# A graph layer's segment sums on TensorE: 256 result columns in place of 128, except in the last ten groups

## The chip, the core and the metric

The kernel runs on one core of a Trainium2 chip. The metric is the device time in microseconds (us) from launch to end of one execution. Before the change three runs took 2691.51, 2695.5 and 2681.98 us; the median is 2691.51 us.

The engines are called by the profile's names: PE is TensorE (its weight loads are PEld), DVE is VectorE, ACT is ScalarE, POOL is GpSimd and SP is SyncE. A "q" behind a name is the engine's sequencer.

## What is computed

One message-passing layer of a graph network, a residual and a layer norm, all in fp32. There are 12500 nodes with 64 features and 212500 edges with 32 features, sorted by destination. Every edge runs through a two-layer MLP, the messages are summed by destination, and every node runs through another MLP:

```python
msg_in = jnp.concatenate([nodes[row], nodes[col], edge_features], axis=-1)
messages = _mlp(msg_in, mW1, mb1, mW2, mb2)
aggregated = jax.ops.segment_sum(messages, col, num_segments=nodes.shape[0])
upd_in = jnp.concatenate([nodes, aggregated], axis=-1)
...
x = _layernorm(x + _L0_gnn_ref(x, src, dst, edge_attr_32, ...), axis=-1)
```

`_mlp` is `relu(x @ W1 + b1) @ W2 + b2`. The kernel sums the hidden layer of the messages (128 wide) by destination and multiplies by `mW2 @ uW1` afterwards, once per node.

## The kernel before, in words

**Groups and tiles.** The edges are cut into 554 groups (`G`) of 384, each of three tiles (`TG`) of 128 edges. Since edges are sorted by destination, all destinations of a group lie in a window of 32 nodes (`W`). Four groups share one block of edge features (`SB`).

**What happens to a group g.**

- `gather` (L142, POOL): one indirect DMA for each tile (L145) fetches the 64 source features of 128 edges into `own.s[g % RING]`. There are 20 such buffers (`RING`). Gathers are issued 16 groups ahead in program order (`AHEAD`), and the first gather of a group waits for ACT's copy of the group 20 earlier (`copy_by[g - RING]`).
- `onehot` (L321, DVE): one comparison (L324) writes a 128x32 matrix of ones and zeros for each tile, saying which node of the window an edge goes to, behind the 64 features in the same buffer.
- `turn` (L354, PE): three transposes (L360) bring features and one-hot matrix to edge-per-column form in PSUM; ACT copies them to `own.st` (L372).
- `hidden` (L381, PE): one matmul for each tile (L392, two instructions each in the profile) makes the hidden layer; ACT applies the ReLU (L401) into `own.h`.
- `sums` (L411, PE): a small transpose (L419), then one matmul for each tile (L422, again two instructions each) that adds the hidden vectors up by destination. The result has 128 hidden rows and 32 columns of nodes; DVE adds it to `agg` (L431) and counts (L432).
- For 52 groups (`COPIED`), the third tile isn't gathered: DVE (L349) or ACT (L350) copies its 128 source columns one by one out of a transposed node table `xc` on the chip, spread over the steps before. Such a group has two gathers in place of three and two more matmuls in `hidden`.

**The repeated columns.** The moving operand of the sums' matmul is the 32-column one-hot matrix, read `TIMES` = 4 times over through a broadcast, so that the result has 4 x 32 = 128 columns, all four copies alike. Only the first copy (`sg[:, 0, :]`) is read. The places behind it in the same PSUM bank, the count line (`TIMES * W`) and the windows' products (`(TIMES + 1) * W`), are set by the same constant.

**Steps.** `step` (L502) puts work of several groups into one uninterrupted stretch on PE. In iteration k of the main loop (L536) it is `turn(k)`, `hidden(k - 2)`, `sums(k - 4)`, in that order. The first instruction of a step waits for all that the step needs, and only the last one signals. On that signal ACT copies group k (L372) and applies the ReLU for k - 2 (L401), and DVE adds the sums for k - 4 (L431, L432). Two PSUM sets (`own.ps[k % 2]`) alternate, so step k waits for what ACT and DVE did with step k - 2, and for `onehot(k)`. Every fourth step ends with one more matmul (`windows`, L310), which DVE copies in four pieces (L315); every fourth iteration also has DVE copy four windows (`places`, L303).

**Order on each engine.** The program is written in the order in which each engine executes it; there is no scheduler. DVE's order in an iteration is `onehot(k + 1)`, the two adds of step k, then any pieces of windows and copied columns. ACT's is copy, ReLU, copied columns. Every 512 nodes, an update (L438 to L483) runs the node MLP between steps: L449, L450 and L462 on PE.

**The end.** In the last ten groups (`SHORT`), the three parts are steps of their own, so that they follow each other without the distance of two iterations.

`unordered` (L584) is a way for inputs that break the assumptions, and isn't executed here.

Of the kernel before, what the change touches and what calls it, by code (L numbers as in the profile page):

```python
# [22 lines left out]
D = 64  # L23
# [5 lines left out]
W = 32  # L29
TG = 3  # L30
GE = TG * P
G = (E + GE - 1) // GE
# [12 lines left out]
SHORT = 10  # L45
# [3 lines left out]
COPIED = {**dict.fromkeys(BY_DVE, (ET.DVE, BY_DVE)), **dict.fromkeys(BY_ACT, (ET.Activation, BY_ACT))}  # L49
SLACK = 3  # L50
REGS = 8
TIMES = 4


def tiles_of(g):

    n = min(GE, E - g * GE)
    return [min(P, n - j * P) for j in range((n + P - 1) // P)]
# [46 lines left out]
def ordered(ctx: ExitStack, tc: tile.TileContext, a, own, ok):  # L105
# [25 lines left out]
    def after(first, *others):  # L131

        tc.declare_no_dep(first.ins, group="quiet", reason="waits for the last of a step")
        for i in others:
            tc.add_manual_dep(
                first.ins, i.ins.name,
                mybir.DependencyInfo(mybir.DependencyClass.Sync, mybir.DependencyReason.DATA),
                reason="the kernel's own rings",
            )
        return first  # L140
# [165 lines left out]
    def windows(b, wp, own_bank=True):  # L306


        xw, n = xws.pop(b)
        did = nc.tensor.matmul(wp[: n * W, :], xw[:, :n, :], w1b, start=True, stop=True)  # L310

        def copies():
            for i in range(n):
                g = b * SB + i
                c = nc.vector.tensor_copy(wm[g % NW][D : D + W, :], wp[i * W : (i + 1) * W, :])  # L315
                after(c, *([did] if own_bank else []), *([hidden_by[g - NW]] if g >= NW else []))
                wm_by[g] = c

        return did, copies
# [91 lines left out]
    def sums(g, ps):  # L411
        h, s = own.h[g % NH], own.s[g % RING]
        sizes = tiles_of(g)
        sg = ps[:, 2, : TIMES * W].rearrange("p (t w) -> p t w", w=W)


        lo = D if sizes[-1] == P else 0
        line = ps[0:1, 2, TIMES * W :][:, : D + W - lo]
        did = [nc.tensor.transpose(line, counts[lo:, g : g + 1], ident[lo : D + W, lo : D + W])]  # L419
        line = line[:, D - lo :]  # L420
        for j, p in enumerate(sizes):
            did.append(nc.tensor.matmul(  # L422
                sg, h[:p, j, :],
                s[:p, j, D:].unsqueeze(1).to_broadcast([p, TIMES, W]),
                start=j == 0, stop=j == len(sizes) - 1))

        def add(step):
            sums_by[g] = step
            at = bass.ds(starts.pop(g), W)
            return [  # L430
                after(nc.vector.tensor_tensor(agg[:, at], sg[:, 0, :], agg[:, at], ALU.add), step),  # L431
                after(nc.vector.tensor_tensor(xc[D : D + 1, at], line,  # L432
                                              xc[D : D + 1, at], ALU.add), step),
            ]

        return did, [*relu_by[g], copy_by[g]], add
# [53 lines left out]
    def step_update(g):  # L490
# [5 lines left out]
        elif now:  # L496
            got = now[1](now[0])
            now = [got, *now[2:]] if len(now) > 2 else []

    users = {part: [[], []] for part in (turn, hidden, sums)}  # L500

    def step(*work):  # L502
# [10 lines left out]
        for part, g, *_ in parts:  # L513
            if part is sums:
                for b in [b for b in xws if (b - 1) * SB <= g][:1]:
                    last, copies = windows(b, own.ps[g % 2][:, 2, (TIMES + 1) * W :][:, :H])
                    did.append(last)
# [18 lines left out]
    for k in range(G):  # L536
        if k < BITS:
            bit(k)
        if k % SB == 2:
            inputs(k // SB + 2)  # L540
        if k % SB == 1:
            places(k // SB + 1)
        onehot(k + 1)
        if k < G - SHORT:
            step((turn, k), *([(hidden, k - 2)] if k > 1 else []),
                 *([(sums, k - 4)] if k > 3 else []))
            made, summed = max(0, k - 1), max(0, k - 3)
        else:

            step((turn, k))  # L550
            for _ in range(2):
                if summed < made:
                    step((sums, summed))
                    summed += 1
            for _ in range(2):
                if made <= k:
                    step((hidden, made))
                    made += 1
        if k + AHEAD < G:
            gather(k + AHEAD)  # L560
        copies_of(k)
# [334 lines left out]
```

## Time and profile before

| | before |
|---|---|
| runs | 2691.51, 2695.5, 2681.98 us |
| profiled execution, its own time | 2690.72 us |
| its span, first to last instruction | 2688.9 us |
| mean granted PE clock | 0.787 |
| PE busy | 1687.1 us, 63% |
| POOL busy | 1519.4 us, 57% |
| DVE busy | 1060.2 us, 39% |
| ACT busy | 827.3 us, 31% |
| sums' matmuls L422 | 3322 instructions, 647.5 us |
| gathers L145 | 1609 instructions, 1518.6 us, 944 ns each |

A span of 2688.9 us over 554 groups is 4.85 us for a group. No engine is busy all the time, so the table alone doesn't say what sets this pace. Matmuls are pipelined: the mean time of one (343 ns) includes its way through the array, so the distance between the starts of two is shorter than that. The view of waits tells what ended the idle time in front of an instruction, and the timeline gives the start of every instruction in us from the start of the span.

### The profile page before, as it was taken

Reading aid. Unit: us, or ns where it says so; the run is one execution under the profiler, and the core shown is the slowest. Engines: PE = TensorE matmul, PEld = TensorE weight load, DVE = VectorE, ACT = ScalarE, POOL = GpSimd, SP = SyncE. Lnnn points to the kernel's source line nnn. Section 1 sums busy time; section 2 is a strip of 40 time slices with the busy share of each in tenths; the row PEclk is TensorE's granted clock in tenths of the full one; section 3 lists DMA queues with packets and bytes.
Section 4 is the critical chain, followed back from the end, with each engine's and each line's share of the span. In section 5 each row is a group of like instructions: output and inputs, shape, how many; then the busy total and the mean of one; then the engine's idle time right before and its main releaser. Section 6 shows DMA issues by size and latency. Waiting matters only on the chain.

```text
span 2688.9 us, 45023 instructions
## 1 busy us (share of the span) xinstructions
PE 1687.1 (63%) x9545; PEld 1457.1 (54%) x9545; DVE 1060.2 (39%) x7163; ACT 827.3 (31%) x4455; POOL 1519.4 (57%) x1616
## 2 busy tenths in 40 slices
PE   1356666666666675766666656666566666677667
PEld 0355555555555565655555555555555555565555
DVE  4124344344443444443434434434344343443423
ACT  0123333333333333333333333333333333333322
POOL 7565555555555555555555555555555555565550
PEclk9777787778777777777777878787777777787779
DMA  3211111111111111111111111111111111111110
GB/s 80 58 44 32 35 32 36 31 36 32 35 37 32 34 34 35 31 36 32 37 31 35 34 32 34 34 34 34 35 32 34 33 37 31 35 35 35 33 34 14
DMA packets 71878, 95.29 MB, mean 35 GB/s; under 512 B 32633, under 2 KB 40076, under 8 KB 71596
## 3 DMA queue, kind: packets, MB, share of 16 engines
q0 software_dynamic: 51488, 52.80, 10.3%
q1 hardware_dynamic: 19193, 39.06, 5.3%
q8 instruction: 81, 1.33, 0.2%
q14 instruction: 202, 1.65, 0.2%
q10 hardware_dynamic: 914, 0.46, 0.1%
HBM read 88.90 MB, written 3.20 MB: 34 GB/s over the span
## 4 chain that ended last, share of the span: by engine, by line
PE 50%; issue 18%; another core or an unknown queue 16%; ACT 10%; ACTq 3%; DVE 3%; DMA 0%; DVEq 0%; SPq 0%
PE own_ps L422 19%; PE own_ps L392 16%; PE own_ps L360 9%; ACT own_h L401 3%; ACT own_f L350 3%; ACT own_st L372 3%; ACTq L343 2%; PE own_ps L419 2%; PE u_ps L462 2%; PE u_ps L449 1%; PE own_ps L310 1%; ACTq L350 1%; PE u_ps L450 1%; DVE agg L431 1%
## 5 line engine op out<-in xcount | busy, mean ns | idle before, releaser
L145 POOL DMA_INDIRECT own_s<-in_x,src_sb x1609 | 1518.6, 944 | 1091.0 <-ACT own_st L372 677.1
L360 PE MATMUL own_ps<-own_ident,own_s 128*96 128x128 f32 x1661 | 364.2, 341 | 906.5 <-issue 677.0
L372 ACT ACTIVATE own_st<-own_ps 96x384 f32<-96x384 f32 (+2 forms) x606 | 286.1, 472 | 1697.7 <-PE own_ps L422 1006.0
L360 PEld LDWEIGHTS own_ps<-own_ident,own_s 128*96 128x96 f32 x1661 | 224.4, 159 | 983.9 <-issue 735.6
L422 PE MATMUL own_ps<-own_s,own_h 128*128 128x128 f32 x3322 | 647.5, 343 | 0.4 <-issue 0.3
L392 PE MATMUL own_ps<-own_wm,own_st 128*128 128x128 f32 (+1 forms) x3322 | 630.8, 338 | 1.4 <-DVE own_wm L315 1.4
L392 PEld LDWEIGHTS own_ps<-own_wm,own_st 128*128 128x128 f32 (+1 forms) x3322 | 571.9, 251 | 16.5 <-issue 11.7
L431 DVE TENSOR_TENSOR agg<-own_ps,agg 128x32 f32 x554 | 105.2, 190 | 1202.7 <-ACT own_h L401 1089.6
L422 PEld LDWEIGHTS own_ps<-own_s,own_h 128*128 128x128 f32 x3322 | 525.6, 236 | 27.3 <-issue 0.3
L349 DVE COPY own_f<-xc 64x1 f32 x3968 | 428.8, 143 | 217.7 <-issue 213.2
L350 ACT ACTIVATE own_f<-xc 64x1 f32 x2688 | 304.6, 193 | 9.1 <-issue 6.2
L401 ACT ACTIVATE own_h<-own_ps 128x384 f32<-128x384 f32 x553 | 263.3, 476 | 18.4 <-PE own_ps L392 13.1
L315 DVE COPY own_wm<-own_ps 32x128 f32<-32x128 f32 x550 | 156.9, 285 | 6.8 <-issue 1.3
L324 DVE TENSOR_TENSOR own_s<-iota,dlc 128x96 f32<-128x96 f32 x554 | 135.7, 245 | 21.6 <-issue 16.7
L432 DVE TENSOR_TENSOR xc<-own_ps,xc 1x32 f32 x554 | 101.2, 183 | 27.8 <-PE u_ps L450 7.4
L419 PE MATMUL own_ps<-own_ident,own_counts 32*1 32x32 f32 x554 | 107.1, 193 | 4.2 <-ACT own_st L372 1.9
L372 ACT ACTIVATION_READ_ACCUMULATOR own_st<-own_ps 96x1 f32 (+1 forms) x554 | 106.4, 192 | 0.6
L303 DVE COPY xw<-xc 66x32 f32 x554 | 78.6, 210 | 49.2 <-issue 48.3
L419 PEld LDWEIGHTS own_ps<-own_ident,own_counts 32*1 32x1 f32 x554 | 41.3, 74 | 93.8 <-issue 47.8
L310 PE MATMUL own_ps<-w1b,xw 66*128 66x128 f32 (+1 forms) x276 | 56.9, 290 | 0.0
L462 PE MATMUL u_ps<-u,u 128*128 128x64 f32 (+1 forms) x196 | 49.1, 398 | 10.0 <-ACT u L452 10.0
L462 PEld LDWEIGHTS u_ps<-u,u 128*128 128x128 f32 (+1 forms) x196 | 47.5, 326 | 11.5 <-ACT u L452 11.3
(63 smaller groups left out, 338.5 us busy)
## 6 DMA issues: line engine op xcount, KB each, us to landing
own_st<-in_efT SPq DMA_DIRECT2D x138, 192.0 KB
own_s<-in_x,src_sb POOLq DMA_INDIRECT x1609
xin<-in_x SPq DMA_DIRECT2D x24, 128.0 KB
out<-o SPq DMA_DIRECT2D x24, 128.0 KB
xc<-in_xT SPq DMA_DIRECT2D x12, 179.2 KB
dlc_i<-in_dst_cols SPq DMA_DIRECT2D x1, 831.0 KB
xc<-in_xT SPq DMA_DIRECT2D x4, 179.5 KB
src_sb<-in_src SPq DMA_DIRECT2D x13, 50.5 KB
```

Of the source, the lines that this page charges most:

```text
L145: nc.gpsimd.indirect_dma_start(out=s[:p, j, :D], out_offset=None, in_=x[:, :], in_offset=bass.IndirectOffsetOnAxis(ap=src_sb[:p, g * TG + ...
L315: c = nc.vector.tensor_copy(wm[g % NW][D : D + W, :], wp[i * W : (i + 1) * W, :])
L324: places_by[g] = nc.vector.tensor_tensor(own.s[g % RING][:, :, D:], iota.unsqueeze(1).to_broadcast([P, TG, W]), dlc[:, g * TG : (g + 1) * ...
L349: c = (nc.vector.tensor_copy(*column) if engine == ET.DVE else nc.scalar.activation(*column, AF.Copy))
L350: else nc.scalar.activation(*column, AF.Copy))
L360: nc.tensor.transpose(xt[:, j * P : j * P + p], s[:p, j, :], ident[:p, :p])
L372: nc.scalar.activation(t[to, c : c + m], xt[to, :m], AF.Copy, **({"accum_out": counts[to, g : g + 1]} if to.stop > D else {})), step)
L392: did.append(nc.tensor.matmul(pre[:p, j, :], edges, weights, start=i == 0, stop=i == len(parts) - 1))
L401: relu_by[g] = [nc.scalar.activation(h, pre, AF.Relu)]
L419: did = [nc.tensor.transpose(line, counts[lo:, g : g + 1], ident[lo : D + W, lo : D + W])]
L422: did.append(nc.tensor.matmul(sg, h[:p, j, :], s[:p, j, D:].unsqueeze(1).to_broadcast([p, TIMES, W]), start=j == 0, stop=j == len(sizes) - 1))
L462: nc.tensor.matmul(o_ps[:p, k], u[:, k:q:n], u2, start=True, stop=True)
```

## The change

The constant goes from four to eight, so the moving operand of the sums' matmul has 256 columns in place of 128. In the last ten groups it stays at 128 columns through a second constant.

```diff
-TIMES = 4
+TIMES = 8
+FEW = 4
...
     def sums(g, ps):
         h, s = own.h[g % NH], own.s[g % RING]
         sizes = tiles_of(g)
-        sg = ps[:, 2, : TIMES * W].rearrange("p (t w) -> p t w", w=W)
+        times = TIMES if g < G - SHORT else FEW
+        sg = ps[:, 2, : times * W].rearrange("p (t w) -> p t w", w=W)
...
                 sg, h[:p, j, :],
-                s[:p, j, D:].unsqueeze(1).to_broadcast([p, TIMES, W]),
+                s[:p, j, D:].unsqueeze(1).to_broadcast([p, times, W]),
```

The count line and the windows' products move with `TIMES`: from column 128 to 256 and from column 160 to 288 of the same bank of 512 columns. The number and the order of the instructions are the same on every engine; 544 of the 554 groups have matmuls of 128x256 in place of 128x128.

## The prediction

> **What bounds the kernel now.** I began with busy time and slices on the page. PE is busy 63% of the span, nothing more, and its clock changes all the time.
>
> ```profile
> PE 1687.1 (63%) x9545; PEld 1457.1 (54%) x9545; DVE 1060.2 (39%) x7163; ACT 827.3 (31%) x4455; POOL 1519.4 (57%) x1616
> ...
> PEclk9777787778777777777777878787777777787779
> ```
>
> The second row is the granted clock in tenths. It is an average of two values: the trace's clock records know only full and half speed, in stretches of 3.4 us or multiples of it. So each PE stage has two prices.
>
> Next the waits: they name a circle in which ACT waits for PE, POOL for ACT, and PE mostly for nothing visible.
>
> ```profile
> ACT own_st L372 <- PE own_ps L422: 1006.0, 245, 8.2
> ...
> POOL own_s L145 <- ACT own_st L372: 677.1, 274, 8.7
> PE own_ps L360 <- issue: 677.0, 223, 10.0
> ```
>
> POOL's 274 waits of 2.5 us are one for each pair of groups. To see what closes the circle I read the timeline of one stretch, engine by engine: start, duration, engine, work, and in brackets the idle time before.
>
> ```profile
> 1037.69 1.65 PE L422 MATMUL own_ps<-own_s,own_h 128*128 128x128 f32 x6
> ...
> 1043.78 0.94 PE L422 MATMUL own_ps<-own_s,own_h 128*128 128x128 f32 x6
> ...
> 1046.41 0.94 PE L422 MATMUL own_ps<-own_s,own_h 128*128 128x128 f32 x6
> 1054.17 0.85 PE L360 MATMUL own_ps<-own_ident,own_s 128*96 128x128 f32 x3 [6.83 <-issue]
> ```
>
> ```profile
> 1046.45 0.94 POOL L145 DMA_INDIRECT own_s<-in_x,src_sb  x1 [0.30 <-issue]
> 1050.34 0.94 POOL L145 DMA_INDIRECT own_s<-in_x,src_sb  x1 [2.94 <-ACT own_st L372]
> ```
>
> ```profile
> 1048.99 0.87 ACT L372 ACTIVATE own_st<-own_ps 64x256 f32<-64x256 f32 x2 [5.48 <-remote]
> ```
>
> The step with the sums at 1043.78 is over at 1044.94, the next one at 1047.35. ACT starts on the first only at 1048.99, 4.05 us late. It isn't busy; PE's semaphore is recorded as rising at 1048.97. That moment is 1.6 us after POOL's last allowed gather ended at 1047.39: when that gather lands. Counted over the trace, of 356 steps where ACT stood waiting, 189 got their signal over 0.3 us late, and 161 of these within 0.2 us after a gather's landing; of 44 steps that ended after the landing of the group 19 ahead, none was late. And where gathers are over (the last is issued at 2610.4), signals come at once:
>
> ```profile
> 2623.83 0.94 PE L422 MATMUL own_ps<-own_s,own_h 128*128 128x128 f32 x6
> ...
> 2625.81 0.94 PE L422 MATMUL own_ps<-own_s,own_h 128*128 128x128 f32 x6
> ```
>
> ```profile
> 2624.80 0.49 ACT L372 ACTIVATE own_st<-own_ps 96x384 f32<-96x384 f32 x1 [1.72 <-PE own_ps L422]
> ...
> 2626.78 0.49 ACT L372 ACTIVATE own_st<-own_ps 96x384 f32<-96x384 f32 x1 [1.02 <-PE own_ps L422]
> ```
>
> There a step takes 1.98 us, against 4.75 in the middle. Why PE's signal waits for a landing I can't say; that it does sets the pace. A pair of groups costs 6 gathers x 1.247 us (start to start) + about 1.45 to the landing + about 0.6 for ACT's copy and POOL's start: 9.5 us. Measured from one pair's signal to the next: median 9.52 and 9.57, and about 8.2 where a copied group leaves five gathers. So **the bound is POOL's ring with its landing**, and PE work costs only where a step ends after the landing.
>
> **Where PE is late.** Steps fall into a rhythm of four. Call them by k mod 4. P (0) and Q (1) run at full clock and wait for the landing: P's signal comes a median 3.8 us after its work, Q's with it. Then PE idles (median 5.6 us before R) and drops to half clock. R (2) runs mostly at half clock (110 of 129 start there): its signal comes 0.0 us after its work in the median, so PE ends about with the landing or after it. S (3) follows at once, turns to full clock on its way, and signals promptly.
>
> **The change, part by part.**
>
> *Columns.* Six L422 instructions start 112 ns apart at full clock and 213 ns at half (1043.78 and 1037.69 above). L449 with 512 columns starts 853 ns apart at half clock, four times the 213 ns: time goes with columns. So 256 columns add 6 x 213 = 1.28 us at half clock and 6 x 112 = 0.67 us, say 0.64, at full. Weighted with the clock that each step had, that is 0.86 us in the mean and 443 us in all. If all of it were on the path: 2690.7 + 443 = 3134 us; if none: 0. The weights (L422 PEld) are as many and as large, and their time stays hidden under the longer matmuls.
>
> *P and Q:* 0.64 us each disappears in the 3.8 us. If this cover went, it would cost 130 x 0.64 = 83 us. Q ends 1.3 us later, still before the signal or just with it.
>
> *R:* I add each R's extra to its end and count only what goes past its present signal: 0.82 us in the mean, 106 us over 129 steps. Two things reduce this. The clock: P and Q end 1.3 us later, so the idle time before R shrinks. Of R's idle times 78 are at least 5 us, 14 are 3 to 5, 37 below; less 1.3 us they are 37, 52 and 40. Above 5 us all started at half clock, between 57%, below 65% (after updates). That makes 37 + 30 + 26 = 93 of 129 in place of 110: 106 x 93/110 = 90 us. And a longer R more often sees the clock rise before its sums end: the rise comes some 3.4 to 6.8 us after a cold start (one full busy stretch), and the added time lies at 3.8 to 5.9 us, so in about 4 of 10 cases it costs half: 90 x 0.8 = 72 us. The 17 R steps that become warm also give back what they now exceed the landing by, about 0.4 us each: -7 us.
>
> *S:* it ends about 1 us later. What waits for it is POOL's next credit, needed 3.7 us after its run starts; S now ends 1 to 3 us into that run. Most stay hidden: 0. If the cover is gone, 72 us (0.56 x 129), counted as for R.
>
> *After the last gather:* some ten steps run at PE's pace, +0.64 each: +6 us. The last ten groups keep 128 columns: 0.
>
> *DVE, ACT, POOL, SP:* same instructions, same order. DVE reads the same 32 columns; the count line and windows move inside their bank. 0; nothing to hide.
>
> Sum: 72 - 7 + 6 = **+71 us, 2690.7 + 71 = about 2762 us**. The profiled execution lies 0.8 us under the median of the runs, which needs no correction. About 0.5%, 13 us, is what a measurement of this kernel can tell from no change.
>
> **A rule that speaks against this.** The row: R starts at half clock after every idle time of 5 us or more, after about half of those of 3 to 5 us. The Trainium skill ("TensorE: Matmul & The Clock Gate", section "Why this matters for your kernels") asks for no PE-idle gaps over about 3 us between bursts, and its Part 1 gives one idle window of about 3.4 us as the reason; longer sums fill such gaps, which would be a gain. By that threshold a gap of 5.6 - 1.3 = 4.3 us stays cold, no R step changes, and the sum would be some 20 us higher; were every gap brought under it, the first rival below holds.
>
> **Rivals.**
>
> *The clock pays for it (faster).* If P's and Q's filling keeps R at full clock in most cases, R falls to 3.0 us, behind the landing, and the interval into R goes from a mean 9.45 us to the ring's 9.52 or 8.25 (with a copied group, 52 of 129): mean 9.0. That gives 0.4 x 129 = 55 us, less 6: 2640 us. It decides from an idle time before R of under some 3 us. For it: 40 of 129 would be under 3 us. Against it: the other two in three would not. Chance 0.17. If the longer sums also let P's signal out in time, up to 3 us in each four steps would go, towards 2300 us; nothing in the trace shows that column counts matter to it. Chance 0.03.
>
> *S is caught by the gathers (slower still).* S now escapes because it ends early in POOL's run; steps that end over 3.7 us into a run of six were all late. If a quarter to a half of the S steps get there, POOL stops after three gathers and loses about 2 us each: 129 x 0.25 to 0.5 x 2 = 65 to 130 us more: 2830 to 2890, say 2855 us. Chance 0.2.
>
> *Nothing to see.* If R's signal is in truth held by a landing too, with PE's end only near it, and POOL's run moves along, the change stays within 13 us: 2695 us. For it: R is the median case with 0.0. Against it: that R ended after the landing is exactly what those 0.0 say. Chance 0.12.
>
> My forecast has the remaining 0.48, with its own range from 2715 to 2810 us.
>
> **How the numbers follow.** Faster by over 0.5%: 0.17 + 0.03 = 0.2. Within: 0.12. Slower: 0.48 + 0.2 = 0.68. The range reaches from the clock's rival, 2650, to S's upper end, 2870; below lie half of the clock rival and the signal's case, above the last part of S's.
>
> **What would show it.** L422 starts 218 to 224 ns apart at full clock and 427 at half. The 274 POOL waits remain, a landing still in front of P's signal, with P's lateness down to some 3.1 us. The granted clock rises from 0.787 to about 0.83. R's interval grows by 0.5 us, P's stays at 9.57. I am wrong if R starts at full clock in most cases, if P's signal comes right after its last matmul, or if POOL's runs break into threes.

## The result, and the profile after

The changed kernel takes a median 2766.48 us (2762.14 to 2777.45, four runs), the kernel before 2690.07 us (2681.98 to 2695.5, four runs). The ratio is 1.0293, with a 95% interval from 1.0252 to 1.0334: slower, by 76 us in the medians. The profiled execution after took 2777.45 us, with a span of 2775.7 us and a mean granted clock of 0.845; it is the slowest of the four, 86.7 us over the profiled one of before. Inserted lines move the numbers: L422 is now L424, L372 is L373, L360 is L361 and L145 is L146.

The page after, busy time and granted clock in tenths:

```profile
PE 1963.4 (71%) x9545; PEld 1572.4 (57%) x9545; DVE 1060.6 (38%) x7163; ACT 829.6 (30%) x4455; POOL 1519.3 (55%) x1616
...
PEclk9688888888888788877889888788888788888988
...
L424 PE MATMUL own_ps<-own_s,own_h 128*128 128x256 f32 (+1 forms) x3322 | 1020.4, 451 | 0.3 <-issue 0.3
```

The sums' matmuls are busy for 1020.4 us in place of 647.5, 373 us more. PE as a whole has only 276 us more (1963.4 against 1687.1): with a longer share at full clock its other work got shorter. And the time grew by 87 us. So 87 of the 373 us show in the time; if other steps gained, more than that lay on the path. DVE, ACT and POOL have what they had.

The waits of after (engine, line, what it waited for: us in total, times, longest):

```profile
ACT own_st L373 <- PE own_ps L424: 1378.8, 304, 8.1
...
POOL own_s L146 <- ACT own_st L373: 751.0, 270, 9.2
PE own_ps L361 <- issue: 607.1, 223, 6.2
```

It is the same circle as before: POOL still stops 270 times for ACT, ACT 304 times for PE's signal, and PE still idles with nothing named in front of it, though never longer than 6.2 us (10.0 before). One round of four steps, P 204 to S 207, in the timeline of PE, then of ACT and of POOL:

```profile
1070.44 1.56 PE L424 MATMUL own_ps<-own_s,own_h 128*128 128x256 f32 x6
1071.84 0.39 PE L311 MATMUL own_ps<-w1b,xw 66*128 66x128 f32 x2
...
1073.27 1.56 PE L424 MATMUL own_ps<-own_s,own_h 128*128 128x256 f32 x6
1080.78 0.85 PE L361 MATMUL own_ps<-own_ident,own_s 128*96 128x128 f32 x3 [5.95 <-issue]
...
1083.70 2.93 PE L424 MATMUL own_ps<-own_s,own_h 128*128 128x256 f32 x6
1086.42 0.85 PE L361 MATMUL own_ps<-own_ident,own_s 128*96 128x128 f32 x3
```

```profile
1075.59 0.87 ACT L373 ACTIVATE own_st<-own_ps 64x256 f32<-64x256 f32 x2 [5.44 <-PE own_ps L424]
...
1086.66 0.49 ACT L373 ACTIVATE own_st<-own_ps 96x384 f32<-96x384 f32 x1 [7.58 <-PE own_ps L424]
```

```profile
1073.12 0.94 POOL L146 DMA_INDIRECT own_s<-in_x,src_sb  x1 [0.30 <-issue]
1076.94 0.94 POOL L146 DMA_INDIRECT own_s<-in_x,src_sb  x1 [2.87 <-ACT own_st L373]
...
1083.18 0.94 POOL L146 DMA_INDIRECT own_s<-in_x,src_sb  x1 [0.30 <-issue]
1087.51 0.94 POOL L146 DMA_INDIRECT own_s<-in_x,src_sb  x1 [3.38 <-ACT own_st L373]
```

P's work ends at 1072.23 (1071.84 + 0.39), but ACT starts on it only at 1075.59, 1.53 us after POOL's gather of 1073.12 ended. So P's and Q's sums, 1.56 us each at full clock, lie in front of a signal that comes later anyhow. Then PE idles for 5.95 us and starts R at half clock: its sums take 2.93 us and end at 1086.63. POOL's last allowed gather ended at 1084.12; 1.5 us later would be 1085.6, and ACT starts at 1086.66, right after R's work. Here PE is late, and POOL stands until 1087.51.

The same, counted for the steps with 24 <= k < 536 (128 of each kind; the interval runs from the signal of the step two before to this step's signal, as ACT's copy shows it; means in us):

| | P before | P after | Q before | Q after | R before | R after | S before | S after |
|---|---|---|---|---|---|---|---|---|
| interval | 9.51 | 9.51 | 8.93 | 8.58 | 9.45 | 10.08 | 10.00 | 10.97 |
| step's duration | 2.63 | 3.07 | 2.37 | 2.81 | 3.92 | 4.90 | 2.86 | 3.10 |
| signal after the end | 3.22 | 2.88 | 2.65 | 1.90 | 0.51 | 0.32 | 0.60 | 0.10 |
| starts at half clock | 21 | 0 | 17 | 2 | 110 | 88 | 92 | 73 |

A round of four steps is P's interval and R's together (or Q's and S's). P's stays, R's grows by 0.63 us, and 0.63 x 128 = 81 us is nearly the whole loss.

The waits name nothing in front of PE, and the prediction left it at that, but the timeline of DVE shows what R waits for. After P's signal (1075.59 here) ACT copies and applies the ReLU; DVE follows 1.63 us after the signal and then works with hardly a stop until R starts:

```profile
1077.22 0.19 DVE L433 TENSOR_TENSOR agg<-own_ps,agg 128x32 f32 x1 [5.50 <-ACT own_h L402]
...
1077.55 1.18 DVE L316 COPY own_wm<-own_ps 32x128 f32<-32x128 f32 x4
1078.76 0.57 DVE L350 COPY own_f<-xc 64x1 f32 x8
1079.66 0.73 DVE L304 COPY xw<-xc 66x32 f32 x4 [0.33 <-issue]
1080.42 0.26 DVE L325 TENSOR_TENSOR own_s<-iota,dlc 128x96 f32<-128x96 f32 x1
```

These are P's adds, the four pieces of `windows`, copied columns, `places`, and last `onehot` for R's own group. It ends at 1080.68, and R's transposes start at 1080.78. In 126 of the 128 rounds R starts 0.1 us after its `onehot` (122 of 128 before), a mean 4.83 us after P's signal (4.99 before). So R's interval is this stretch, R's own work and what its signal adds: 4.83 + 4.90 + 0.32 = 10.05 of 10.08 us. That is how R comes to be late. What less work of DVE's in that place would gain wasn't tried.

### The profile page after: what moved, and what is told of

It reads as the page before. It is cut to its first block, busy times and chain, and to the rows that moved or that the text cites. A ratio compares the mean times of both kernels' runs of the same rounds, so it can differ in the third digit from the quotient of the medians.

```text
span 2775.7 us, 45023 instructions
## 1 busy us (share of the span) xinstructions
PE 1963.4 (71%) x9545; PEld 1572.4 (57%) x9545; DVE 1060.6 (38%) x7163; ACT 829.6 (30%) x4455; POOL 1519.3 (55%) x1616
## 4 chain that ended last, share of the span: by engine, by line
PE 63%; issue 15%; ACT 8%; another core or an unknown queue 4%; ACTq 2%; DVE 2%; DVEq 0%
PE own_ps L424 32%; PE own_ps L393 15%; PE own_ps L361 9%; ACT own_st L373 3%; ACT own_h L402 2%; ACT own_f L351 2%; PE own_ps L421 2%; PE u_ps L464 2%; ACTq L344 2%; PE own_ps L311 1%; ACTq L351 1%; PE u_ps L451 1%; PE u_ps L452 1%; DVE agg L433 0%
## 5 line engine op out<-in xcount | busy, mean ns | idle before, releaser
L146 POOL DMA_INDIRECT own_s<-in_x,src_sb x1609 | 1518.5, 944 | 1174.0 <-ACT own_st L373 751.0
L424 PE MATMUL own_ps<-own_s,own_h 128*128 128x256 f32 (+1 forms) x3322 | 1020.4, 451 | 0.3 <-issue 0.3
L361 PE MATMUL own_ps<-own_ident,own_s 128*96 128x128 f32 x1661 | 336.6, 320 | 728.9 <-issue 607.1
L373 ACT ACTIVATE own_st<-own_ps 96x384 f32<-96x384 f32 (+2 forms) x606 | 286.5, 473 | 1788.6 <-PE own_ps L424 1378.8
L424 PEld LDWEIGHTS own_ps<-own_s,own_h 128*128 128x128 f32 x3322 | 680.4, 220 | 113.4
L361 PEld LDWEIGHTS own_ps<-own_ident,own_s 128*96 128x96 f32 x1661 | 210.3, 149 | 880.8 <-issue 724.2
L393 PE MATMUL own_ps<-own_wm,own_st 128*128 128x128 f32 (+1 forms) x3322 | 572.7, 315 | 0.7 <-DVE own_wm L316 0.7
L393 PEld LDWEIGHTS own_ps<-own_wm,own_st 128*128 128x128 f32 (+1 forms) x3322 | 514.5, 229 | 14.9 <-issue 10.6
L373 ACT ACTIVATION_READ_ACCUMULATOR own_st<-own_ps 96x1 f32 (+1 forms) x554 | 106.3, 192 | 0.6
L311 PEld LDWEIGHTS own_ps<-w1b,xw 66*128 66x128 f32 (+1 forms) x276 | 54.2, 197 | 7.9
```

What stands on the lines that cost most here:

```text
L146: nc.gpsimd.indirect_dma_start(out=s[:p, j, :D], out_offset=None, in_=x[:, :], in_offset=bass.IndirectOffsetOnAxis(ap=src_sb[:p, g * TG + ...
L361: nc.tensor.transpose(xt[:, j * P : j * P + p], s[:p, j, :], ident[:p, :p])
L373: nc.scalar.activation(t[to, c : c + m], xt[to, :m], AF.Copy, **({"accum_out": counts[to, g : g + 1]} if to.stop > D else {})), step)
L393: did.append(nc.tensor.matmul(pre[:p, j, :], edges, weights, start=i == 0, stop=i == len(parts) - 1))
L424: did.append(nc.tensor.matmul(sg, h[:p, j, :], s[:p, j, D:].unsqueeze(1).to_broadcast([p, times, W]), start=j == 0, stop=j == len(sizes) - 1))
```

## The experiments

A group's sums run in the step with k four higher, so g mod 4 is the kind of step. Those of the first set give times against the kernel before at 2690.7 us; the runs fell on a chip where it takes another time, so the ratio to the kernel before on the same chip is what counts.

### The added columns in some kinds of steps only

```diff
-        times = TIMES if g < G - SHORT else FEW
+        times = TIMES if g < G - SHORT and g % 4 in (0, 1) else FEW
```

and the same with `(2, 3)`, `== 2` and `== 3`. The kernel before took 2658.28 us on this chip.

P and Q:

> 256 columns only in the sums of groups with g mod 4 of 0 and 1 (the steps P and Q), 128 in all others. Theory (the landing of the gathers covers P and Q, only R pays): 2670 to 2695 us, with P still signalling 3 us after its work and R starting somewhat warmer. Rival (PE's added time is on the path wherever it stands, in proportion): half of the 76 us, about 2728 us.

Measured: 2655.89 us, ratio 0.9992 (0.9972 to 1.0012). No cost, as the theory has it.

R and S:

> 256 columns only where g mod 4 is 2 or 3 (R and S). Theory: all of the cost and none of the warmer clock, 2765 to 2790 us. Rival (in proportion): about 2728 us.

Measured: 2759.82 us, ratio 1.0362 (1.0317 to 1.0408).

R alone:

> 256 columns only where g mod 4 is 2 (R). Theory: nearly all of the cost with a quarter of the added work, 2755 to 2785 us; the interval into R grows by over 0.5 us. Rival (in proportion): 19 us, about 2709 us.

Measured: 2759.86 us, ratio 1.0385 (1.036 to 1.041). That is over the range that I expected, whose upper end is 1.035 times 2690.7 us.

S alone:

> 256 columns only where g mod 4 is 3 (S). Theory: 2680 to 2700 us, since nothing waits for S. Rival (S ends later, its signal falls among the gathers or POOL runs out of credit): over 2720 us. Rival in proportion: about 2709 us.

Measured: 2645.9 us, ratio 0.9951 (0.9933 to 0.9969).

A quarter of the added work, in R, brings all of the loss; the other three quarters bring none, alone or in pairs. With R alone it is even more than what the whole change costs (1.0385 against 1.0293, in different sets of runs). The timelines of the kernel with R alone, of PE, ACT and POOL, show why:

```profile
1080.11 0.39 PE L311 MATMUL own_ps<-w1b,xw 66*128 66x128 f32 x2
...
1082.16 0.94 PE L424 MATMUL own_ps<-own_s,own_h 128*128 128x128 f32 x6
1088.36 0.85 PE L361 MATMUL own_ps<-own_ident,own_s 128*96 128x128 f32 x3 [5.26 <-issue]
...
1090.55 2.93 PE L424 MATMUL own_ps<-own_s,own_h 128*128 128x256 f32 x6
```

```profile
1084.02 0.49 ACT L373 ACTIVATE own_st<-own_ps 96x384 f32<-96x384 f32 x1 [4.83 <-PE own_ps L424]
...
1093.52 0.49 ACT L373 ACTIVATE own_st<-own_ps 96x384 f32<-96x384 f32 x1 [6.69 <-PE own_ps L424]
```

```profile
1091.10 0.94 POOL L146 DMA_INDIRECT own_s<-in_x,src_sb  x1 [0.30 <-issue]
1094.36 0.94 POOL L146 DMA_INDIRECT own_s<-in_x,src_sb  x1 [2.31 <-ACT own_st L373]
```

P ends at 1080.50 and its signal is taken at 1084.02, 3.5 us late, with 128 columns as with 256. R's sums end at 1093.48, ACT starts at 1093.52 and POOL at 1094.36, after 2.31 us without a gather. Without longer P and Q, 117 of 128 R steps start at half clock, and 119 with R and S; 88 did with the whole change. That is the clock's repayment: the counts show it, though the whole change wasn't run in this set beside them, and it is the smaller part.

Why S alone is 0.5% faster isn't settled. R's interval is 9.49 us there and 9.28 with P and Q alone, P's 9.15 and 9.37: the sums of the two agree within 0.01 us.

### R's sums shortened, and what holds PE's signal

On the chip of this set the kernel before took 2036.34 us (2035.65 to 2039.13, 13 runs), 24% less than 2690.07. The first kernel has 32 columns in R and 128 elsewhere:

```diff
-        times = TIMES if g < G - SHORT else FEW
+        times = 1 if g < G - SHORT and g % 4 == 2 else FEW
```

> 32 columns in the sums of R (g mod 4 of 2) alone, 128 in all others. Theory: R already ends about with the landing, so a shorter R gains only where it is over: 5 to 25 us less than before. Rival (R's length is on the path both ways, by the same amount that 256 columns added): 70 to 100 us less.

Measured: 2037.6 us, ratio 1.001 (1.0 to 1.0019). No gain. The reason is in its waits:

```profile
ACT own_st L373 <- PE own_ps L424: 808.9, 370, 6.2
...
POOL own_s L146 <- issue: 370.6, 1216, 0.3
```

No wait of POOL's for ACT is longer than 0.3 us, the usual stop between two gathers: POOL works without a break, 1609 x 1.247 us = 2006 us of the 2034.4 us span. PE's signals come within 0.3 us of the work's end in 491 of 512 steps; in the other 21 ACT was still at its own work. The lateness that my theory starts from doesn't exist in this run, and POOL's work fills it, so R couldn't matter.

Two kernels leave the gathers away after the first 20 groups:

```diff
+        if g >= RING:
+            loads[g] = []
+            return
```

With 128 columns:

> The gathers after the first 20 groups are left out, so later groups work on old features; sums with 128 columns. Theory (PE's signals wait for landings of gathers): every signal within 0.1 us of its work, P included; no ring, so 1900 to 2100 us. Rival (P's signal is late because of what PE does at full clock): P still signals 3 us late and the time stays over 2500 us.

One run gave 1988.56 us. With 256 columns:

> The same without gathers after the first 20 groups, sums with 256 columns. Theory: prompt signals too; now the longer sums are on the path of every step that PE sets, 80 to 250 us more than with 128 columns. Rival: over 2500 us.

One run gave 2105.34 us. And SP's plain transfers in place of POOL's gathers:

```diff
-            nc.gpsimd.indirect_dma_start(
-                out=s[:p, j, :D], out_offset=None, in_=x[:, :],
...
+            nc.sync.dma_start(s[:p, j, :D], x[(r := (g * TG + j) * P % (N - P)) : r + p, :])
```

> In place of each gather SP issues a plain transfer of 128 rows of x in order (the rows are not those of the edges), into the same buffer, with the same waits; sums with 128 columns. Theory as narrowed: if it is POOL's gathers that hold PE's signals, they become prompt and the time goes to 1900 to 2200 us. If any landing in the ring of buffers does it, signals stay late and the time follows the transfers, over 2300 us.

One run gave 2002.36 us. No signal is late in any of the three. Since none is late with gathers either, they don't tell what holds PE's signal. They give a pace without POOL's gathers: 1988.56 us with 128 columns, 117 us more with 256, each from one run on this chip.

### The change on a chip with prompt signals

In the last set, on one more chip, the kernel before took 2037.63 us (2036.01 to 2038.58, 13 runs). The change itself:

> The change itself again, beside the kernel before on the same chip. If on this chip PE's signals wait for gather landings (the kernel before takes some 2650 to 2700 us): only R gets longer, by about 0.63 us x 128 = 81 us, so 1.025 to 1.04 times the time before. If they don't (the kernel before takes some 2036 us): POOL's gathers end close behind PE, and 256 columns make PE the bound; without gathers they took 2105.34 us, so 2105 to 2150 us, 1.034 to 1.055 times. Rival, that the lock swallows nothing and columns cost the same everywhere: with no lock 1.00 to 1.02, since POOL would still set the pace.

Measured: 2092.22 us, ratio 1.0261 (1.0238 to 1.0283); under the 2105 us and the 1.034 expected, over the rival's 1.02. And 256 columns everywhere but in R (`g % 4 != 2`):

> 256 columns in groups whose sums fall in P, Q and S, 128 in R: three quarters of the added work, none of it in R. My theory, if signals wait for landings here: no cost, 0 to 20 us less than before (P and Q alone were at 0.9992 times, S alone at 0.9951). Rival, that the columns cost by their number: three quarters of what the change costs, 55 to 75 us more than before. If signals don't wait here (before some 2036 us): PE is the bound with three quarters of the 117 us above 1988.56, so 2075 to 2115 us.

Measured: 2037.87 us, ratio 1.0002 (0.9993 to 1.0012). That is 37 us under what I expected for this kind of chip. The chain that ended last, first of the change and then of the kernel without it in R:

```profile
PE 78%; issue 8%; ACT 7%; DVE 3%; ACTq 2%; DMA 1%; SPq 0%; DVEq 0%
```

```profile
PE 63%; issue 11%; DMA 7%; ACT 6%; DVE 5%; POOL 5%; ACTq 2%; DVEq 1%; SPq 0%; POOLq 0%
```

With the change PE has 78% of the chain and POOL no part in it; without it in R, POOL and its DMAs are in it. There POOL issues its last gather at 2011.7 of 2035.6 us and the span ends 23.9 us later; with the change it is issued at 2022.3 and another 71.4 us go by for the groups that POOL had run ahead. Signals are prompt with the change too; PE, then ACT:

```profile
1167.43 0.39 PE L311 MATMUL own_ps<-w1b,xw 66*128 66x128 f32 x2
...
1172.20 0.50 PE L361 MATMUL own_ps<-own_ident,own_s 128*96 128x128 f32 x3 [1.21 <-ACT own_h L402]
```

```profile
1167.85 0.49 ACT L373 ACTIVATE own_st<-own_ps 96x384 f32<-96x384 f32 x1 [1.41 <-PE own_ps L311]
```

P ends at 1167.82 and ACT starts at 1167.85. In all 491 steps for which ACT stood waiting (again 24 <= k < 536), the signal came at once, and a gather was in flight each time.

My sum for three quarters of the columns started from the other chip's 1988.56 us; on this one the same kernel without gathers takes 1962.15 us (below), and that is 26 of the 37 us. The clock speaks for the rest, though no run separates it. Beside the gatherless kernel with 128 columns on this chip, P, Q and S are longer by 0.45 to 0.58 us (means), but R takes 2.64 us in place of 3.06, and ends at half clock in 29 of 128 cases in place of 63. With the change R takes 3.46 us, and a pair of P and R 14.94 us in place of 14.43. So once the other three quarters are there, R's quarter brings all of the 54 us on this chip too. Whether it would alone isn't shown: how far PE stays under POOL's pace without it, a chain that POOL closes doesn't tell, and R alone wasn't run here.

The two kernels about the signal once more:

> The kernel before with 128 columns, in which the gathers after the first 20 groups are left out, so that it works on old features. If signals wait for gather landings here: the lateness is gone in all four kinds of steps, and the time is 1960 to 2030 us, as on the chip without late signals (1988.56). Rival, that signals are late on this chip for another reason, such as ACT or DVE taking them up slowly: lateness stays, over 2300 us. If the kernel before takes some 2036 us here: 1988 us again, and nothing is told apart.

> The kernel before with 128 columns, in which SP issues a plain transfer of 128 rows of x in their order in place of each gather, so that the features are others but as many bytes come as late. If it is the landing of POOL's gather that holds PE's signal: no lateness, 1980 to 2060 us. Rival, that any transfer into the buffers of features holds it until it lands: lateness stays near 3 us in P, over 2400 us. If the kernel before takes some 2036 us here: 2002 us again, and nothing is told apart.

One run of each gave 1962.15 and 2003.06 us. With the kernel before at 2037.63 us, nothing is told apart again.

## Why the prediction was right, point by point

**What bounds the kernel**: the circle of waits, with signals late until about a gather's landing, held in the first runs and in the first set of experiments, and only there. One link was missing from it, ACT's and DVE's work between P's signal and R's start, which puts R's end behind the landing. In 358 steps of the kernel before ACT stood waiting; 187 signals were over 0.3 us late, and the middle half of these came between 1.40 and 1.52 us after the end of a gather. After the change it is 154 of 383, and 1.44 to 1.54 us. In the profiles from the chips of the two later sets, not one waiting step was late while gathers ran.

**P and Q at nothing**: held. P's interval is 9.51 us before and after; its lateness fell from a median 3.79 to 3.32 us (about 3.1 foretold). In the mean its duration grew by 0.44 us, of which lateness took 0.34. With the columns there alone the ratio is 0.9992.

**R, 72 less 7 = 65 us**: the right step, a bit small: 81 us. Matmuls cost as counted: at full clock they mostly start 212 to 220 ns apart, at half 424 to 428 ns (six take 1.56 and 2.93 us). The clock repaid about as counted, 88 starts at half clock (93 foretold, 110 before), though in another way, and that the count came out so near is luck: PE's idle time before R shrank from a median 5.57 to 5.08 us, not by 1.3 us, so 70 stayed at 5 us or more (37 foretold), and what helped is that fewer short idle times ended at half clock (5 of 29 under 3 us; before, 24 of 37). The rise before the sums end was sized about right: 30 of the 88 R steps that start at half clock end at full (4 in 10 foretold). What I took too low is how much of R's extra shows: its duration grew by 0.98 us in the mean, lateness gave back 0.19 us, an earlier start after P's signal some 0.16 us (4.99 to 4.83 us), and 0.63 us remained where I had 65/129 = 0.50.

**S at nothing**: held, and S is even at 0.9951 alone. Its 0.60 us of lateness went to 0.10, and POOL's stops stayed one for a pair of groups (270; 274 before), mostly with six gathers between two of them.

**After the last gather, +6 us**: 82.5 us in place of 78.6, +3.9 us.

**The sum**: 81 + 4 = 85 of the 86.7 us between the two profiled executions. The granted clock is 0.845, not 0.83.

**The rivals.** *The clock pays* fell in the first runs: R starts at half clock in 88 of 128 cases. On the last chip a part of it shows: with 256 columns in P, Q and S, R ends at full clock in 99 of 128 cases (65 in the kernel without gathers), and the time stays at POOL's pace. *The signal comes in time* fell: P's is late by 3.32 us. *S is caught* fell with S alone. *Nothing to see* fell with R alone, +3.85%.

**The rule on idle gaps.** Of R's idle times of 5 us and more 79 of 79 ended at half clock before and 64 of 70 after; of those from 3 to 5 us, 8 of 14 and 19 of 31. The Trainium skill ("TensorE: Matmul & The Clock Gate", section "Why this matters for your kernels") asks for no idle gap over about 3 us. These counts agree with a limit there that isn't sharp: such a gap is a risk of about one in two, not a switch.

**Open**: what holds PE's signal back. It goes with the end of gathers in the first runs, where a gather's landing in the 1.4 to 1.5 us after its end would be the simplest cause. A gather in flight isn't enough for it: before the change all 187 late signals had one in flight, from POOL's start on it to its last DMA packet, when the work ended, but so had 115 prompt ones (after: 154 and 135), and on the last chip all 491 prompt ones. The kernels that were to tell POOL's gathers from other transfers ran only on chips without lateness. Whether the lateness belongs to a chip or to the time of the runs can't be told (for the first runs the chip isn't on record), and the version without R's columns wasn't tried where signals are late.

## What to carry to other kernels

Added work is priced by the step that it lies in: count for each kind of step how long after its end the next engine takes it up, and only steps taken up at once can cost anything. In a rhythm with one cold step, put work into the warm steps in front of it, where it is hidden and keeps the clock up, and none into the cold one. When the waits name nothing in front of an engine, look at the other engines' timelines just before: here it was DVE, 0.1 us earlier. And read the bound on the chip where the time is measured: here the bound was another one on two of the chips, and the same edit cost the same few per cent for another reason.

## What was not expected of the hardware

The kernel before took 2690 and 2658 us in the first two sets of runs, and 2036 and 2038 us on the chips of the two later ones. A gather takes POOL 944 to 945 ns on all of them. What differs in the profiles is PE's signal: a median 3.79 us late in P in the first runs, and prompt where the times are near 2036 us, in the kernel with a shorter R, and in the change itself. But it isn't PE's signal alone. The traces with late signals hold 7421 to 8960 records of semaphore updates by gathers for the same 1609 gathers, those with prompt ones about 25,600, and those of the engines' own updates are fewer too (4227 before, 5701 with the shorter R). So updates are delivered or recorded in another way there; which of the two, and whether it makes the lateness, no run shows. The Trainium skill ("Perfetto Trace Analysis", section "Tensor Engine Instruction (MATMUL, LD_WEIGHTS)") says that a matmul's end in the profile is computed and that its semaphore update comes after it, outside the profile. These runs agree that the signal comes after the computed end, and show that it can come 3 to 4 us after; whether that is this tail or something else that holds the signal stays open.

A quarter of the change's work cost more than all of it, 1.0385 against 1.0293 where signals were late, though in two sets of runs. That work in P and Q is repaid by a warmer R (88 cold starts in place of 117) would explain it.
